# A convolution inside a fused two-layer kernel: taps clipped to the image in place of a zero border, with another spread of TensorE's work over the stages

## The chip, the cores and the metric

The kernel runs on one core of a Trainium2 chip. The core has a matrix engine (TensorE, PE in the profile; its weight loads are listed apart as PEld), three engines for elementwise work (VectorE or DVE, ScalarE or ACT, GpSimd or POOL), an engine that only issues transfers (SyncE or SP), and DMA queues. Matmuls write to PSUM, an accumulation memory that TensorE, VectorE and ScalarE can use; everything else lies in SBUF, and both have 128 partitions. The metric is the device time of one execution in microseconds (us).

## What is computed

The input x holds 32 images of 256 channels and 32 x 32 pixels, in fp32. Two layers follow, each one normalized first and added to its input:

```python
# cut to what matters; _gn is a GroupNorm of 32 groups (8 channels each) over channels of a group and all pixels
x = x + conv3x3(_gn(x), weight, bias)        # 256 -> 256 channels, padding 1; operands rounded to fp16, result rounded to fp16
                                             # (the kernel works per image, each on its own)
h = _gn(x)                                   # second layer, an involution
y = relu(bn(w1 @ h))                         # 256 -> 64 channels
w = w2 @ y + b2                              # 49 weights for each pixel and each of 16 groups
x = x + sum over the 7 x 7 taps of w[tap, group] * h[pixel + tap]     # zero outside of the image
```

The convolution of one image is, for each half of the rows (nt) and each half of the output channels (mh), a sum of 18 matmuls: 9 taps times 2 halves of the input channels (kh). Each has 128 x 128 weights and up to 512 columns, which are 16 rows of 32 pixels.

## The kernel before

Work is cut into stages: one stage is an image b, a block k of 8 rows (four blocks), a set v of columns of the 7 x 7 window (two sets), and a set d of its rows (two sets), so 16 stages per image. In a stage VectorE and GpSimd multiply the involution's weights with shifted pixels, and TensorE sums these products one stage later. Beside this, the "front" of a later image goes on in small steps: it is a Python generator, and each `yield` ends what it does in one stage. A front takes over 30 stages, so the fronts of two or three images are under way at once.

```python
xq = const.tile([P, CH, H0, H0], F16, name="xq")      # H0 = 34: a border of one pixel
nc.gpsimd.memset(xq, 0.0)
...
MORE = 1
CONV = (0, 9, 0, 9)                                   # matmuls in each of four stages

def front(b):
    ...                                               # sums, means, squares, variances of the first norm
    gn.apply(lambda h: xq[:, h, PAD0 : PAD0 + H, PAD0 : PAD0 + W], xt)        # ScalarE (L243)
    yield
    ...
    for s in range(1, 4 * len(units) + 3):            # units: (nt, mh), four of them
        u, i = divmod(s, 4)
        if u < len(units):
            nt, mh = units[u]
            if i == 1:
                pc = ps_c.tile([P, NT], F32, tag="pc", name="pc")
            for n in range(sum(CONV[:i]), sum(CONV[: i + 1])):
                kh, k = divmod(n, K0 * K0)
                i0, j0 = divmod(k, K0)
                nc.tensor.matmul(                     # L288
                    pc,
                    wq[:, kh, k, mh * P : (mh + 1) * P],
                    xq[:, kh, nt * RT + i0 : nt * RT + i0 + RT, j0 : j0 + W],
                    start=n == 0, stop=n == CH * K0 * K0 - 1,
                )
        ...                                           # a stage after a unit's last matmul: q (VectorE, L302), qb (ScalarE, L304);
                                                      # then x += qb (GpSimd, L306), then the unit's sum (ScalarE)
        yield
    gn.means()                                        # group means: matmuls into pg (L203)
    gn.squares(xt)                                    # ScalarE
    yield
    yield
    gn.variances()                                    # pg again
    yield
    gn.scales()                                       # reciprocal on VectorE
    gn.apply(lambda h: xn[:, h]..., xt)               # xn, ScalarE (L231 to L243)
    yield
    for r in range(0, H // 4, 2):
        ...                                           # four 128 x 128 transposes of xn into pt (L326), a copy (L330), four transfers
        if r % 4 == 0:
            yield MORE                                # go on in this stage, after the other fronts
        else:
            yield
            if r == 2:
                yield
    load_pixels(b, 0)
    yield
    ...                                               # projection to y: matmuls into py (L346), ReLU on ScalarE (L354)
    yield
...
# in each stage, in this order: products of this stage (VectorE, GpSimd; L417), sums of the stage before (TensorE; L471),
# the end of a block (ScalarE copy L482, transposes back L488, addition on VectorE L497, L500),
# in every second stage the involution's weights for two stages on (pw, TensorE; L380; a copy for GpSimd, ws, ScalarE L389), then:
for b in list(fronts) * 2:
    due = n - FRONT - b * per + 1
    ...
    while b in fronts and done[b] < due:
        got = next(fronts[b], fronts)
        if got is fronts:
            fronts.pop(b)
        elif got == MORE:
            break
        done[b] += 1
```

The sums and the involution's weights are matmuls with 32 output columns, four side by side in the array (in the profile 128*32, 96*32 and 65*32). Convolution, transposes and group means use all 128 columns (128*128), and the projection 64.

Of the kernel before, what the change touches and what calls it, by code (L numbers as in the profile page):

```python
# [8 lines left out]
F16 = mybir.dt.float16  # L9
# [4 lines left out]
P = 128  # L14
B, C, H, W = 32, 256, 32, 32
N = H * W
NT = 512
RT = NT // W
CH = C // P
K0, PAD0 = 3, 1  # L20
H0 = H + 2 * PAD0
K1, PAD1 = 7, 3
TAPS = K1 * K1
CR = 64
# [33 lines left out]
def tile_quant_conv_then_involution(  # L58
# [15 lines left out]
    nc = tc.nc  # L74
    PSUM = bass.MemoryType.PSUM

    const = ctx.enter_context(tc.tile_pool(name="const", bufs=1))
# [9 lines left out]
    def load_x(b):  # L87
        xt = xpool.tile([P, CH, N], F32, tag="x", name=f"x_{b}")
        for h in range(CH):
            nc.sync.dma_start(xt[:, h], x[b, h * P : (h + 1) * P])  # L90
        return xt
# [49 lines left out]
            )  # L141
        shift.append(s)

    xq = const.tile([P, CH, H0, H0], F16, name="xq")
    nc.gpsimd.memset(xq, 0.0)
    eps = const.tile([P, 1], F32, name="eps")
    nc.gpsimd.memset(eps, GN_EPS)
    three_halves = const.tile([P, 1], F32, name="three_halves")
# [99 lines left out]
                    scale=rstd[:, one],  # L248
                )

    MORE = 1

    CONV = (0, 9, 0, 9)

    def front(b):


        xt = x_tiles[b]
        gn = GroupNorm()
        gn.begin(1)  # L260
        for h in range(CH):
            gn.add_up(xt, 0, h, 0, N, AF.Identity)
        yield
        gn.means()
        gn.squares(xt)
        yield
        yield
        gn.variances()
        yield
        gn.scales()  # L270
        yield
        yield

        gn.apply(lambda h: xq[:, h, PAD0 : PAD0 + H, PAD0 : PAD0 + W], xt)
        yield
        gn = GroupNorm()
        gn.begin(N // NT)
        units = [(nt, mh) for nt in range(N // NT) for mh in range(CH)]
        for s in range(1, 4 * len(units) + 3):
# [3 lines that stand above are left out]
                if i == 1:  # L283
                    pc = ps_c.tile([P, NT], F32, tag="pc", name="pc")
                for n in range(sum(CONV[:i]), sum(CONV[: i + 1])):
                    kh, k = divmod(n, K0 * K0)
                    i0, j0 = divmod(k, K0)
                    nc.tensor.matmul(  # L288
                        pc,
                        wq[:, kh, k, mh * P : (mh + 1) * P],  # L290
                        xq[:, kh, nt * RT + i0 : nt * RT + i0 + RT, j0 : j0 + W],
                        start=n == 0,
                        stop=n == CH * K0 * K0 - 1,
                    )

            u, i = divmod(s - 4, 4)
            if 0 <= u < len(units) and i < 3:
                nt, mh = units[u]
                cols = slice(nt * NT, (nt + 1) * NT)
                if i == 0:  # L300
                    q = work.tile([P, NT], F16, tag="q", name="q", bufs=1)
                    nc.vector.tensor_scalar(q, pc, F16_MAX, -F16_MAX, ALU.min, ALU.max)  # L302
                    qb = work.tile([P, NT], F32, tag="qb", name="qb", bufs=1)
                    nc.scalar.activation(qb, q, AF.Identity, bias=bias_sb[:, mh : mh + 1])  # L304
                elif i == 1:
                    nc.gpsimd.tensor_tensor(xt[:, mh, cols], qb, xt[:, mh, cols], ALU.add)  # L306
                else:
                    gn.add_up(xt, nt, mh, nt * NT, (nt + 1) * NT, AF.Identity)
            yield
        gn.means()  # L310
        gn.squares(xt)
        yield
        yield
        gn.variances()
        yield
        gn.scales()
        xn = work.tile([P, CH, N], F32, tag="xn", name=f"xn_{b}", bufs=1)
        gn.apply(lambda h: xn[:, h].rearrange("p (r c) -> p r c", c=W), xt)
        yield

        xd = pixels[b] = dram.tile([W, H, C], F32, tag="xd", name=f"xd_{b}")
        for r in range(0, H // 4, 2):
            pt = ps_m.tile([P, 2, C], F32, tag="m", name="pt")
            for s in range(2):
                for h in range(CH):
                    nc.tensor.transpose(  # L326
                        pt[:, s, h * P : (h + 1) * P], xn[:, h, (r + s) * P : (r + s + 1) * P], ident
                    )
            xt4 = work.tile([P, 2, C], F32, tag="xt4", name="xt4")
            nc.scalar.copy(xt4, pt)  # L330
            for i in range(4):
                nc.sync.dma_start(xd[:, 4 * r + i : 4 * r + i + 5 : 4, :], xt4[i * W : (i + 1) * W])

            if r % 4 == 0:
                yield MORE
            else:
                yield
                if r == 2:
                    yield
        load_pixels(b, 0)  # L340
        yield

        py = ps_m.tile([P, NT], F32, tag="m", name="py")
        for kh in range(CH):
            for nt in range(N // NT):
                nc.tensor.matmul(  # L346
                    py[nt * CR : (nt + 1) * CR],
                    w1_sb[:, kh, :],
                    xn[:, kh, nt * NT : (nt + 1) * NT],
                    start=kh == 0,  # L350
                    stop=kh == CH - 1,
                )
        for nt in range(N // NT):
            nc.scalar.activation(  # L354
                y_pad[b % 2][:CR, nt * RT : (nt + 1) * RT, PAD1 : PAD1 + W],
                py[nt * CR : (nt + 1) * CR].rearrange("p (r c) -> p r c", c=W),
                AF.Relu,
                bias=bn_shift,
                scale=bn_scale,
            )  # L360
        yield

    def load_pixels(b, i):

        for r0, r1 in (((0, 7), (15, 22), (7, 15)), ((0, 14), (14, 22)))[i]:
            src = HELD[i][r0]
            for q in range(Q):
                nc.sync.dma_start(
                    xpix[i][q * W : (q + 1) * W, r0:r1], pixels[b][:, src : src + r1 - r0, :]
                )  # L370
# [146 lines left out]
    with tc.manual_schedule():  # L517
        fronts, done = {}, {}
        ending = iter(())
        acc = last = None  # L520
        pws = {}
        for n in range(FRONT, len(stages) + 3):
            if 0 <= n < len(stages):
                b, k, v, d = stages[n]
                now = stages[n], products(b, k, v, d, *pws[n // 2])
            else:
                now = None
            if last is not None:
                (b, k, v, d), prods = last
                if (v, d) == (0, 0):  # L530
                    acc = ps_acc.tile([P, NT], F32, tag="acc", name="acc")
                sums(acc, v, d, prods)
            next(ending, None)
            if last is not None and (v, d) == (len(COLS) - 1, len(DI) - 1):
                ending = finish(b, k, acc)
                next(ending)
            last = now
            b, at = divmod(n, per)
            if at == 0 and 0 <= b < B:
                load_pixels(b, 1)  # L540
            if 0 <= n + 2 < len(stages) and n % 2 == 0:
                pws.pop(n // 2 - 1, None)
                pws[n // 2 + 1] = weights(*stages[n + 2][:3])
            b, at = divmod(n - LOAD, per)
            if at == 0 and 0 < b < B:
                x_tiles[b] = load_x(b)
            b, at = divmod(n - FRONT, per)
            if at == 0 and 0 <= b < B:
                fronts[b] = front(b)
                done[b] = 0  # L550
            for b in list(fronts) * 2:
                due = n - FRONT - b * per + 1
                if b == 1:

                    due = min(due, max(0, 2 * (due - HOLD)))
                while b in fronts and done[b] < due:
                    got = next(fronts[b], fronts)
                    if got is fronts:
                        fronts.pop(b)
                    elif got == MORE:  # L560
                        break
                    done[b] += 1


# [34 lines left out]
```

## Time and profile before

| | |
|---|---|
| time, median of 3 runs | 2789.55 us (2781.03 to 2789.92) |
| span of the profiled execution | 2788.2 us |
| granted TensorE clock, mean | 0.990 |
| sums (L471), matmul records | 14080 |
| convolution (L288) | 2304 matmuls, 556.3 us busy |
| involution weights (L380) | 14336 records, 440.7 us busy |
| VectorE products (L417) | 2006.3 us and 334.9 us |
| GpSimd products (L417) | 704 instructions, 2407.2 us |
| GpSimd additions (L306) | 128 instructions, 164.5 us, 184.6 us idle ahead of them |
| DMA | 292.60 MB, mean 105 GB/s |

Groups of matmuls overlap in time, so their busy times may not be added. An fp32 matmul leaves two records. "Idle before" is the time in which an engine stood still just ahead of the instructions of a group; what ended it is named behind the arrow. Matmuls are pipelined, and their ends are modelled: the distance from one start to the next says what a matmul costs in a stream, while its length says how long it is under way.

### The profile page before, as it was taken

What the parts mean: (1) busy time and instruction counts of PE and PEld (TensorE: products, weight loads), DVE (VectorE), ACT (ScalarE), POOL (GpSimd) and SP (SyncE); (2) the same over time, 40 slices, a digit from 0 to 9 for tenths busy, and PEclk for the clock granted to TensorE, in tenths of its full rate; (3) what the DMA queues carried; (4) which work ended last, traced back from release to release, by engine and by line L of the source; (5) the groups of instructions that cost most, each with busy time, mean ns of one, the idle gap of its engine ahead of it and who ended that gap; (6) DMA issues with size and microseconds to landing.
All of it is one profiled execution on the core that took longest, in us unless ns stands there. A gap on an engine that the chain in (4) does not pass through costs nothing.

```text
span 2788.2 us, 73320 instructions
## 1 busy us (share of the span) xinstructions
PE 2685.1 (96%) x32320; PEld 1323.7 (47%) x32320; DVE 2484.6 (89%) x1451; ACT 1052.4 (38%) x2179; POOL 2575.8 (92%) x857
## 2 busy tenths in 40 slices
PE   4899999999999999999999999999999999999998
PEld 2444455454444444545444444444444444554443
DVE  1699999999999999999999999999999999999898
ACT  5434343433343433343333333343433343434220
POOL 2799999999999999999999999999999999999997
PEclk8999999999999999999999999999999999999999
DMA  2555343454343454343554343554344553434440
GB/s 84 121 122 117 95 105 93 114 126 112 92 113 85 118 130 108 89 112 89 122 129 101 87 112 98 122 129 93 95 103 107 122 119 94 104 90 101 111 115 16
DMA packets 99853, 292.60 MB, mean 105 GB/s; under 512 B 21389, under 2 KB 62349, under 8 KB 86990
## 3 DMA queue, kind: packets, MB, share of 16 engines
q1 hardware_dynamic: 99534, 287.93, 42.4%
q8 instruction: 252, 4.13, 0.7%
q14 instruction: 67, 0.55, 0.1%
HBM read 220.73 MB, written 67.11 MB: 103 GB/s over the span
## 4 chain that ended last, share of the span: by engine, by line
PE 85%; ACT 10%; issue 2%; POOL 1%; DMA 1%; DVE 1%; POOLq 0%; SPq 0%; ACTq 0%; DVEq 0%
PE acc L471 46%; PE pc L288 18%; PE pw L380 13%; ACT xn L243 3%; PE pt L326 2%; PE py L346 2%; PE acc L488 2%; ACT xq L243 1%; POOL pg L417 1%; ACT w L234 1%; PE pg L203 1%; ACT off L242 1%; ACT rstd L241 1%; ACT qb L304 1%; ACT u L236 1%
## 5 line engine op out<-in xcount | busy, mean ns | idle before, releaser
L417 POOL TENSOR_TENSOR pg<-ws,xpix 96x2048 f32<-96x2048 f32 (+2 forms) x704 | 2407.2, 3452 | 14.5 <-PE acc L471 4.8
L417 DVE TENSOR_TENSOR pa<-pw,xpix 128x4096 f32<-128x4096 f32 (+7 forms) x832 | 2006.3, 2446 | 216.1 <-PE acc L471 171.6
L471 PE MATMUL acc<-pa,shift 128*32 128x512 f32 (+3 forms) x7680 | 1563.8, 569 | 7.9 <-DVE pa L417 7.8
L471 PE MATMUL acc<-pg,shift 128*32 128x512 f32 (+1 forms) x5248 | 1503.2, 599 | 5.5 <-POOL pg L417 5.5
L471 PEld LDWEIGHTS acc<-pa,shift 128*32 128x32 f32 (+1 forms) x7680 | 394.9, 110 | 558.8 <-issue 497.8
L288 PE MATMUL pc<-xq,wq 128*128 128x512 f16 x2304 | 556.3, 387 | 15.6 <-ACT xq L243 10.7
L471 PEld LDWEIGHTS acc<-pg,shift 128*32 128x32 f32 (+1 forms) x5248 | 457.1, 111 | 162.0 <-issue 141.5
L471 PE MATMUL acc<-pb,shift 128*32 128x512 f32 (+1 forms) x1152 | 532.4, 599 | 1.5 <-DVE pb L417 1.5
L380 PEld LDWEIGHTS pw<-w_sb,y 65*32 65x32 f32 x14336 | 413.2, 110 | 139.9 <-issue 133.8
L380 PE MATMUL pw<-w_sb,y 65*32 65x112 f32 x14336 | 440.7, 259 | 0.0
L389 ACT COPY ws<-pw 128x448 f32<-128x448 f32 (+1 forms) x256 | 135.7, 530 | 693.5 <-PE pw L380 507.3
L288 PEld LDWEIGHTS <-wq 128*128 128x128 f16 x2304 | 221.2, 100 | 300.8 <-issue 81.5
L306 POOL TENSOR_TENSOR x<-qb,x 128x512 f32<-128x512 f32 x128 | 164.5, 1285 | 184.6 <-ACT qb L304 171.7
L417 DVE TENSOR_TENSOR pb<-pw,xpix 128x1536 f32<-128x1536 f32 x192 | 334.9, 1744 | 0.0
L482 ACT COPY ob<-acc 128x512 f32<-128x512 f32 x128 | 74.9, 585 | 435.6 <-PE acc L471 434.3
L330 ACT COPY xt<-pt 128x512 f32<-128x512 f32 x128 | 75.0, 586 | 221.9 <-PE pt L326 125.7
L195 ACT ACTIVATE junk<-x 128x512 f16<-128x512 f32 (+1 forms) x192 | 148.1, 771 | 10.0 <-POOL x L306 5.6
L195 ACT ACTIVATE junk<-x,mean 128x1024 f16<-128x1024 f32 x128 | 147.1, 1149 | 4.1
L326 PE MATMUL pt<-ident,xn 128*128 128x128 f32 x512 | 86.8, 283 | 47.4 <-ACT xn L243 45.3
L302 DVE TENSOR_SCALAR q<-pc 128x512 f16<-128x512 f32 x128 | 87.4, 683 | 48.8 <-PE pc L288 48.8
L471 PEld LDWEIGHTS acc<-pb,shift 128*32 128x32 f32 (+1 forms) x1152 | 111.8, 110 | 7.8 <-DVE pb L417 4.2
L220 ACT ACTIVATE s<-pg,eps 128x2 f32<-128x2 f32 x64 | 16.8, 262 | 238.5 <-PE pg L203 238.5
(51 smaller groups left out, 1023.9 us busy)
## 6 DMA issues: line engine op xcount, KB each, us to landing
xpix<-xd SPq DMA_DIRECT2D x256, 256.0 KB, 10.1
xpix<-xd SPq DMA_DIRECT2D x256, 224.0 KB, 5.6
xpix<-xd SPq DMA_DIRECT2D x128, 448.0 KB, 6.9
x<-in_x SPq DMA_DIRECT2D x64, 512.0 KB, 3.6
xd<-xt SPq DMA_DIRECT2D x512, 64.0 KB, 1.7
out<-x SPq DMA_DIRECT2D x32, 640.0 KB, 3.1
out<-x SPq DMA_DIRECT2D x32, 384.0 KB, 2.5
wf<-in_w SPq DMA_DIRECT2D x2, 1152.0 KB, 8.5
```

What stands on the lines that cost most here:

```text
L195: nc.scalar.activation(junk[:, n0:n1], src[:, h, n0:n1], func, bias=bias, accum_out=self.sums[:, part, h : h + 1])
L243: nc.scalar.activation(dst(h), src[:, h].rearrange("p (r c) -> p r c", c=W), AF.Identity, bias=off[:, one], scale=rstd[:, one],)
L288: nc.tensor.matmul(pc, wq[:, kh, k, mh * P : (mh + 1) * P], xq[:, kh, nt * RT + i0 : nt * RT + i0 + RT, j0 : j0 + W], start=n == 0, stop=n ...
L302: nc.vector.tensor_scalar(q, pc, F16_MAX, -F16_MAX, ALU.min, ALU.max)
L306: nc.gpsimd.tensor_tensor(xt[:, mh, cols], qb, xt[:, mh, cols], ALU.add)
L326: nc.tensor.transpose(pt[:, s, h * P : (h + 1) * P], xn[:, h, (r + s) * P : (r + s + 1) * P], ident)
L330: nc.scalar.copy(xt4, pt)
L380: nc.tensor.matmul(pw[q * W : (q + 1) * W, r // 4, o : o + K1 * G], y_pad[b % 2][:, ROWS[k][r], s : s + W], w2_sb[:, dj, :], start=True, s ...
L389: nc.scalar.copy(ws[:p], pw[:p, 1, : 4 * K1 * G].rearrange("p (r m) -> p r m", r=4))
L417: eng.tensor_tensor(o, win, xin, ALU.mult)
L471: nc.tensor.matmul(acc[t * W : (t + 1) * W, cols], shift[v][:p], moving, start=(v, d, i) == (0, 0, 0), stop=(v, d, i) == (len(COLS) - 1, l ...
L482: nc.scalar.copy(ob, acc.rearrange("p (r c) -> p r c", c=C))
```

## The change

The border of zeros around the normalized fp16 input xq goes, with its clearing. Each of the nine taps now covers only those pixels whose input lies inside of the image: a tap that looks up or down leaves out one row in the half that has that edge, a tap that looks left or right leaves out one column (its matmul has rows of 31). The order of the taps changes so that the first and the last of the 18, which start and end the accumulation, are the middle tap, which covers all pixels.

With it comes another spread of the front's work. The 18 matmuls of a unit are issued as 6, 4 and 8 in three stages, not as 9 and 9 in two. The variances come one stage after the squares, not two; the transposes come one group per stage in four stages, not two groups in each of two stages; the projection comes in the stage of the pixel loads, one earlier; and the loop over the fronts is simpler.

```diff
@@ -18,7 +18,6 @@
 RT = NT // W
 CH = C // P
 K0, PAD0 = 3, 1
-H0 = H + 2 * PAD0
 K1, PAD1 = 7, 3
 TAPS = K1 * K1
 CR = 64
@@ -141,8 +140,7 @@
             )
         shift.append(s)
 
-    xq = const.tile([P, CH, H0, H0], F16, name="xq")
-    nc.gpsimd.memset(xq, 0.0)
+    xq = const.tile([P, CH, H, W], F16, name="xq")
     eps = const.tile([P, 1], F32, name="eps")
     nc.gpsimd.memset(eps, GN_EPS)
     three_halves = const.tile([P, 1], F32, name="three_halves")
@@ -248,9 +246,8 @@
                     scale=rstd[:, one],
                 )
 
-    MORE = 1
-
-    CONV = (0, 9, 0, 9)
+
+    CONV = (0, 6, 4, 8)
 
     def front(b):
 
@@ -264,14 +261,14 @@
         gn.means()
         gn.squares(xt)
         yield
-        yield
         gn.variances()
         yield
         gn.scales()
         yield
         yield
-
-        gn.apply(lambda h: xq[:, h, PAD0 : PAD0 + H, PAD0 : PAD0 + W], xt)
+        yield
+
+        gn.apply(lambda h: xq[:, h], xt)
         yield
         gn = GroupNorm()
         gn.begin(N // NT)
@@ -283,12 +280,17 @@
                 if i == 1:
                     pc = ps_c.tile([P, NT], F32, tag="pc", name="pc")
                 for n in range(sum(CONV[:i]), sum(CONV[: i + 1])):
-                    kh, k = divmod(n, K0 * K0)
-                    i0, j0 = divmod(k, K0)
+
+
+                    k = n if n < K0 * K0 else CH * K0 * K0 - 1 - n
+                    kh, k = n // (K0 * K0), (k + K0 * K0 // 2) % (K0 * K0)
+                    di, dj = k // K0 - PAD0, k % K0 - PAD0
+                    r0, r1 = max(nt * RT, -di), min((nt + 1) * RT, H - di)
+                    c0, c1 = max(0, -dj), min(W, W - dj)
                     nc.tensor.matmul(
-                        pc,
+                        pc.rearrange("p (r c) -> p r c", c=W)[:, r0 - nt * RT : r1 - nt * RT, c0:c1],
                         wq[:, kh, k, mh * P : (mh + 1) * P],
-                        xq[:, kh, nt * RT + i0 : nt * RT + i0 + RT, j0 : j0 + W],
+                        xq[:, kh, r0 + di : r1 + di, c0 + dj : c1 + dj],
                         start=n == 0,
                         stop=n == CH * K0 * K0 - 1,
                     )
@@ -310,7 +312,6 @@
         gn.means()
         gn.squares(xt)
         yield
-        yield
         gn.variances()
         yield
         gn.scales()
@@ -330,15 +331,8 @@
             nc.scalar.copy(xt4, pt)
             for i in range(4):
                 nc.sync.dma_start(xd[:, 4 * r + i : 4 * r + i + 5 : 4, :], xt4[i * W : (i + 1) * W])
-
-            if r % 4 == 0:
-                yield MORE
-            else:
-                yield
-                if r == 2:
-                    yield
+            yield
         load_pixels(b, 0)
-        yield
 
         py = ps_m.tile([P, NT], F32, tag="m", name="py")
         for kh in range(CH):
@@ -548,17 +542,14 @@
             if at == 0 and 0 <= b < B:
                 fronts[b] = front(b)
                 done[b] = 0
-            for b in list(fronts) * 2:
+            for b in list(fronts):
                 due = n - FRONT - b * per + 1
                 if b == 1:
 
                     due = min(due, max(0, 2 * (due - HOLD)))
                 while b in fronts and done[b] < due:
-                    got = next(fronts[b], fronts)
-                    if got is fronts:
+                    if next(fronts[b], fronts) is fronts:
                         fronts.pop(b)
-                    elif got == MORE:
-                        break
                     done[b] += 1
```

## The prediction

> **What bounds the kernel now.** I read the page's shares first, then the chain of work that ended last, then the costliest groups.
>
> ```profile
> PE 2685.1 (96%) x32320; PEld 1323.7 (47%) x32320; DVE 2484.6 (89%) x1451; ACT 1052.4 (38%) x2179; POOL 2575.8 (92%) x857
> ...
> PE 85%; ACT 10%; issue 2%; POOL 1%; DMA 1%; DVE 1%; POOLq 0%; SPq 0%; ACTq 0%; DVEq 0%
> PE acc L471 46%; PE pc L288 18%; PE pw L380 13%; ACT xn L243 3%; PE pt L326 2%; PE py L346 2%; PE acc L488 2%; ACT xq L243 1%; POOL pg L417 1%; ACT w L234 1%; PE pg L203 1%; ACT off L242 1%; ACT rstd L241 1%; ACT qb L304 1%; ACT u L236 1%
> ...
> L326 PE MATMUL pt<-ident,xn 128*128 128x128 f32 x512 | 86.8, 283 | 47.4 <-ACT xn L243 45.3
> ```
>
> TensorE carries the chain, GpSimd and VectorE are close behind, and one wait stands out: the pixel transposes (L326) wait 45.3 us in all for the normalized input xn. A busy TensorE need not be one at its peak, so I looked at the steady state. The projection (py, L346) starts 84.21 us after that of the image before, image after image. One such period, by busy time of each engine and by what TensorE waited for:
>
> ```profile
> 1200.00:1284.20 84.20, 82.76 (x1016) 41.23 (x1012) 77.49 (x46) 32.78 (x68) 80.15 (x27) 1.00 0.44 107
> PE pt L326 <- ACT xn L243: 1.4, 1, 1.4
> ```
>
> The first line's columns after the length are PE, PEld, DVE, ACT and POOL. TensorE has no idle time in a period but 1.4 us, all of it that wait. So the time is 32 times TensorE's work in a period, plus this wait, plus a start of 77 us before the first projection and a tail of about 104 us after the last. VectorE (77.5) and GpSimd (80.2) fit in, GpSimd with 4 us to spare.
>
> What TensorE's work consists of is seen in the timeline of TensorE (start, length, instructions):
>
> ```profile
> 1214.09 0.59 PE L471 MATMUL acc<-pg,shift 128*32 128x512 f32 x1
> 1214.61 0.66 PE L488 MATMUL acc<-ident,ob 128*128 128x128 f32 x4
> 1215.10 0.28 PE L203 MATMUL pg<-sums,avg 128*128 128x2 f32 x2
> 1215.24 2.14 PE L288 MATMUL pc<-xq,wq 128*128 128x512 f16 x9
> 1217.32 0.62 PE L471 MATMUL acc<-pa,shift 128*32 128x512 f32 x2
> ...
> 1224.47 0.90 PE L471 MATMUL acc<-pg,shift 96*32 96x512 f32 x2
> 1225.30 0.33 PE L326 MATMUL pt<-ident,xn 128*128 128x128 f32 x1
> 1227.01 0.55 PE L326 MATMUL pt<-ident,xn 128*128 128x128 f32 x3 [1.38 <-ACT xn L243]
> 1227.39 2.15 PE L288 MATMUL pc<-xq,wq 128*128 128x512 f16 x9
> 1229.38 0.60 PE L326 MATMUL pt<-ident,xn 128*128 128x128 f32 x4
> 1229.91 0.62 PE L471 MATMUL acc<-pa,shift 96*32 96x512 f32 x2
> ```
>
> Work on all 128 columns (transposes, group means, convolution) comes in islands between sums and weights that use the array as four strips of 32 columns. The starts of single records give what an island costs beside its work. Within the sums the last record of a row of eight is followed after 409 ns; before an island after 523 to 525, so 115 ns are lost going in. A convolution matmul is followed by the next after 217 ns, but by the sums after 309, so 92 are lost going out: **207 ns per island**. An island that begins with a transpose loses 56 more (165 instead of 109 ns after the first).
>
> The nine matmuls of a convolution run show a second thing. Median distances to the next start are 216, 229, 215, 216, 229, 216, 215, 229 ns: the taps whose rows begin at an odd column (j0 = 1) cost 13 ns more. Sixteen rows of one extra fp16 pair are 32 elements, 6% of 512, and 6% of 213 ns is 13. So rows seem to be charged by pairs touched: 17 instead of 16.
>
> **What the Trainium skill says.** "TensorE: Matmul & The Clock Gate", Back-to-back issue gap: N/2.4 + 2.5 ns for a warm matmul alone, 215.8 for 512 columns; the trace has 216, so the convolution is charged by its columns, and the page says nothing of the 229. "TensorEngine Tiling (Array Packing)", Key Properties: "Changing tiling mode (not just tile) drains the TensorE"; the 115 + 92 ns agree. "PSUM — Partial Sum Buffer", Specifications: an 8-byte line, and any non-contiguous access pattern slows matmuls significantly. That bears on the new outputs of 31 columns; here L488 writes runs of 32 with gaps for three blocks in four and takes 109 ns between starts either way, but no run in this trace starts at an odd column.
>
> **The change part by part.**
>
> *Clipped taps.* A run is nine taps on half an image; there are 8 runs per image (2 halves, 2 output halves, 2 input halves). Three taps of a run lose one row of 16: 32 of 512 columns, 13 ns each, 40 ns. The three middle taps, at an odd column because of the border, now begin at column 0: 229 to 216, 39 ns. The six side taps have rows of 31, which still touch 16 pairs, so I count no gain for them; counted by element it would be 6 x 16 columns, 39 ns more. Sum: 79 ns x 8 = -0.63 us per image, **-20 us** over 32 (-30 by element).
>
> *More islands.* Nine taps in each of two stages become 6, 4 and 8 in three, and transposes and group means no longer share a stage with convolution in each case. Counting islands along the two instruction orders: 254 before, 466 after, 212 more; in the steady state 8 and 15 per image. The seven are four short convolution runs, one of transposes alone and two of group means alone. 212 x 0.207 = 43.9 us; two more islands per image begin with transposes, 64 x 0.056 = 3.6. All of it is on TensorE, which has no idle time to hide it: **+47.5 us**.
>
> *The xn wait.* Before, xn is computed in the stage just ahead of the first transposes: ScalarE waits for the copy of the weights (ends 1222.2), needs 4.75 us for the scales and the two halves of xn (ends 1226.95), and TensorE is there at 1225.3. After, the variances come a stage earlier, and so do scale and xn; in the frame of this period VectorE's reciprocal can come at 1215.1, right after its products, and xn is done at 1220.0. The transposes are one stage earlier too, but behind 2.6 us of sums and 1.6 us of weights of that stage, at about 1221.2. Margin 1.2 us, so the wait goes: **-45 us**. This is a choice: I trust the queues to keep their present leads.
>
> *No border, no clearing of it, dense xq.* One memset of 2 us at the start, beside other work; the ScalarE write of xq is off the path. The start changes by 2 us at most, the tail not at all, as it has no convolution.
>
> Sum: -20 + 47.5 - 45 = -17.5 us; from 2789.6 to **2772**. Per image that is 83.6 us.
>
> Does GpSimd allow it? Its products for one stage ended at most 0.3 us ahead of the sums three times in the period I followed. Moving every stage's start by the figures above, the work of GpSimd between two additions of the convolution result (21.4, 21.4, 18.7, 18.8 us) meets TensorE stretches of 21.8, 23.2, 20.4 and 18.3. It falls behind by 0.5 us in one, has it back in the next two, and no product comes late, with 0.2 us to spare at the tightest. VectorE's tightest is 0.8. I add no wait but widen the range upward.
>
> **Rivals.**
>
> *Odd columns slow the output.* A tap with input one column to the left writes columns 1 to 31, from input that starts even, so every pair straddles two lines. That is a third of the convolution, 768 matmuls. If each line were written twice, each would take some 200 ns more: +154 us, about 2926. For it: the page on PSUM. Against: an odd input start to an even output costs only 13 ns today, so pairs can be shifted somewhere. I give it one in ten.
>
> *The wait stays in another place*: xn late again, or means and variances (a stage closer together) held up by ScalarE's squares, or products from GpSimd. One wait of 1.4 us per image leaves the gain of the clipping against the islands: about 2817. For it: GpSimd's small lead. Against: squares take 2.3 us plus a mean, and 4 us of TensorE work lie between.
>
> *Islands overlap better than counted*: the new ones follow weights rather than sums, and the loss going in may differ there. At half of the count: 2749.
>
> **Range and chances.** The three terms are each uncertain by 10 to 15 us; most of the weight lies between a side gain by element (2762) and a small new wait. I take 2752 to 2806. A change by 2% is 56 us: down to 2734 all must go well at once, 0.03; up to 2845 needs the odd columns, or the wait to come back doubled, 0.11; within, 0.86.
>
> **What will show it.** Starts of the convolution's matmuls: 216 for full taps, 202 for those of 15 rows, 216 for rows of 31 (209 if by element, over 300 if the odd column hurts). Islands: 15 per image with 115 and 92 ns around them. The L326 wait on xn: near zero. A projection every 83.6 us. I am wrong if an interval over 230 ns shows up in the convolution, or if TensorE has idle time at pg, pt, or the sums.

## The result and the profile after

The changed kernel takes **2762.44 us** (median of 6; 2760.99 to 2764.09) against 2789.58 for the kernel before: a ratio of 0.9908, 95% interval 0.9895 to 0.9921. The prediction was 2772, range 2752 to 2806. From the page of the kernel after, the shares, and the chain of work that ended last by engine and by line:

```profile
PE 2700.3 (98%) x32320; PEld 1226.3 (44%) x32320; DVE 2472.5 (90%) x1451; ACT 1047.1 (38%) x2179; POOL 2572.9 (93%) x856
...
PE 90%; ACT 5%; POOL 2%; DVE 1%; issue 1%; POOLq 0%; DMA 0%; SPq 0%; ACTq 0%; DVEq 0%
PE acc L465 50%; PE pc L290 18%; PE pw L374 14%; PE pt L327 2%; PE py L340 2%; PE acc L482 2%; POOL pg L411 2%; PE pg L201 2%; ACT xq L241 1%; DVE pa L411 1%; ACT qb L306 1%; ACT w L232 1%; ACT junk L193 1%; ACT rstd L239 0%; ACT u L234 0%
```

TensorE is busy longer (2700 in place of 2685 us) in a shorter span, and ScalarE's xn (3% before) is no longer among the lines of the chain that the page lists. The groups by line show where the wait went; the column behind the last bar is the idle time ahead of the group:

```profile
L290 PE MATMUL pc<-xq,wq 128*128 128x496 f16 (+3 forms) x2304 | 556.9, 380 | 18.5 <-ACT xq L241 15.2 <-DVE q L304 3.3
L327 PE MATMUL pt<-ident,xn 128*128 128x128 f32 x512 | 82.2, 283 | 1.1 <-ACT xt L331 1.1
```

The pixel transposes wait 1.1 us in place of 47.4. In a steady period (columns as in the prediction: length, then PE, PEld, DVE, ACT, POOL):

```profile
1061.60:1145.22 83.62, 83.46 (x1014) 37.99 (x1011) 77.11 (x46) 32.60 (x68) 80.17 (x27) 1.00 0.45 109
```

And all that TensorE waited for in another period:

```profile
PE pc L290 <- ACT xq L241: 0.2, 1, 0.2
```

The projection returns every 83.62 us. The timeline of TensorE in the stage where the transposes begin:

```profile
1121.38 1.72 PE L374 MATMUL pw<-w_sb,y 65*32 65x112 f32 x64
1123.03 0.66 PE L327 MATMUL pt<-ident,xn 128*128 128x128 f32 x4
1123.52 1.00 PE L290 MATMUL pc<-xq,wq 128*128 128x480 f16 x4
1124.45 0.62 PE L465 MATMUL acc<-pa,shift 96*32 96x512 f32 x2
```

Transposes and four matmuls of the convolution follow the weights in one island, and the four transposes run without a break.

Busy time hides part of the waits, as the ends of matmuls are modelled. So I kept a ledger: for each matmul record of TensorE the distance to the start of the next, added up by what the record is, over 24 steady images. It sums to the period, with waits in it.

| us per image | before | after | clip alone (exp. 1) | spread alone (exp. 1) | early variances (exp. 2) | clip + early variances (exp. 6) |
|---|---|---|---|---|---|---|
| sums | 47.22 | 46.85 | 47.54 | 46.85 | 46.88 | 47.19 |
| involution weights | 12.05 | 12.98 | 12.05 | 12.98 | 12.24 | 12.24 |
| convolution | 16.26 | 16.31 | 15.63 | 16.94 | 16.26 | 15.63 |
| transposes to pixels | 3.59 | 2.01 | 3.43 | 2.01 | 1.99 | 1.99 |
| transposes of a block | 2.19 | 2.29 | 2.04 | 2.30 | 2.20 | 2.03 |
| group means | 1.03 | 1.30 | 1.03 | 1.30 | 1.20 | 1.20 |
| projection | 1.87 | 1.87 | 1.87 | 1.87 | 1.87 | 1.87 |
| period | 84.21 | 83.62 | 83.58 | 84.25 | 82.63 | 82.15 |

The loss going into an island is booked with the record ahead of it, so more islands show under weights too. Before to after: the transposes lose 1.58 us, which is the wait; the convolution loses 0.63 of columns and gains 0.68 of loss going out; weights, means and block transposes gain 1.30; the sums lose 0.37. Together -0.59 us per image.

### The profile page after: what moved, and what is told of

Its sections match the earlier page's. It is cut to its first block, busy times and chain, and to the rows that moved or that the text cites. A ratio compares the mean times of both kernels' runs of the same rounds, so it can differ in the third digit from the quotient of the medians.

```text
span 2761.9 us, 73318 instructions
## 1 busy us (share of the span) xinstructions
PE 2700.3 (98%) x32320; PEld 1226.3 (44%) x32320; DVE 2472.5 (90%) x1451; ACT 1047.1 (38%) x2179; POOL 2572.9 (93%) x856
## 4 chain that ended last, share of the span: by engine, by line
PE 90%; ACT 5%; POOL 2%; DVE 1%; issue 1%; POOLq 0%; DMA 0%; SPq 0%; ACTq 0%; DVEq 0%
PE acc L465 50%; PE pc L290 18%; PE pw L374 14%; PE pt L327 2%; PE py L340 2%; PE acc L482 2%; POOL pg L411 2%; PE pg L201 2%; ACT xq L241 1%; DVE pa L411 1%; ACT qb L306 1%; ACT w L232 1%; ACT junk L193 1%; ACT rstd L239 0%; ACT u L234 0%
## 5 line engine op out<-in xcount | busy, mean ns | idle before, releaser
L465 PE MATMUL acc<-pg,shift 128*32 128x512 f32 (+1 forms) x5248 | 1480.8, 599 | 6.1 <-POOL pg L411 6.1
L465 PEld LDWEIGHTS acc<-pa,shift 128*32 128x32 f32 (+1 forms) x7680 | 380.2, 110 | 802.8 <-issue 748.5
L290 PE MATMUL pc<-xq,wq 128*128 128x496 f16 (+3 forms) x2304 | 556.9, 380 | 18.5 <-ACT xq L241 15.2
L465 PEld LDWEIGHTS acc<-pg,shift 128*32 128x32 f32 (+1 forms) x5248 | 357.3, 110 | 63.4 <-issue 49.4
L290 PEld LDWEIGHTS <-wq 128*128 128x128 f16 x2304 | 215.2, 100 | 293.9 <-issue 119.3
L482 PEld LDWEIGHTS acc<-ident,ob 128*128 128x128 f32 x512 | 53.6, 140 | 108.1 <-issue 82.1
L306 ACT ACTIVATE qb<-q,bias_sb 128x512 f32<-128x512 f16 x128 | 92.5, 723 | 10.6 <-DVE q L304 10.6
```

The lines of the kernel that those rows point to most:

```text
L290: nc.tensor.matmul(pc.rearrange("p (r c) -> p r c", c=W)[:, r0 - nt * RT : r1 - nt * RT, c0:c1], wq[:, kh, k, mh * P : (mh + 1) * P], xq[: ...
L465: nc.tensor.matmul(acc[t * W : (t + 1) * W, cols], shift[v][:p], moving, start=(v, d, i) == (0, 0, 0), stop=(v, d, i) == (len(COLS) - 1, l ...
L482: nc.tensor.transpose(po[:, h, :, r, :], ob[:, r, h * P : (h + 1) * P], ident)
```

## The experiments

**1. The two parts apart.** First the clipped taps in the old stages:

```diff
# kernel before, plus only:
-    xq[:, kh, nt * RT + i0 : nt * RT + i0 + RT, j0 : j0 + W]     (border of zeros; CONV stays (0, 9, 0, 9))
+    xq[:, kh, r0 + di : r1 + di, c0 + dj : c1 + dj]               (dense xq, output rows and columns cut likewise, taps in the new order)
```

> The kernel before with clipped taps alone; stages as before (9 and 9, eight islands of 128-column work per image). My theory: only the convolution's columns change, so a projection every 84.21 - 0.63 = 83.58 us, the wait of the first transposes for xn stays at 1.4 us per image, time 2769 us. Rival: a TensorE that is faster only waits longer for xn, the wait grows to 2.0 us, and the time stays at 2789.

Measured: 2767.36 us (ratio 0.9945, 0.9925 to 0.9964), period 83.58. The convolution lost just the 0.63 us. TensorE's waits in a period of this kernel:

```profile
PE pt L328 <- ACT xn L242: 1.2, 1, 1.2
```

So the wait stays, a little shorter. The transposes lost 0.16 us and the block transposes 0.15; the sums gained as much (47.22 to 47.54).

Then the spread alone, with the border put back:

```diff
# kernel after, but
-    xq = const.tile([P, CH, H, W], F16, name="xq")               (clipped taps)
+    xq = const.tile([P, CH, H0, H0], F16, name="xq")             (zero border, nine full taps in the old order)
```

> The changed kernel with the zero border and full taps put back; 6, 4, 8 and 15 islands per image stay. My theory: the islands cost 1.56 us per image and the wait for xn is gone, so a projection every 84.25 us; with the shorter start of the changed kernel, 2782 us. If the shorter start comes from the clipped taps and not from the order of stages, 2790.

Measured: 2784.32 us (0.9994, 0.9985 to 1.0004), period 84.25. In the steady state the spread is worth nothing: 1.58 us of wait are exchanged for 1.62 us of islands and other rows of the ledger. The gain of the change per image is that of the clipped taps.

**2. The wait by itself.** Only the second norm's variances are moved:

```diff
         gn.squares(xt)
         yield
-        yield
         gn.variances()
         ...
         gn.apply(lambda h: xn[:, h]..., xt)
         yield
+        yield
```

> The kernel before with one thing moved: the second norm's variances, scales and xn come one stage earlier, the transposes stay where they were. My theory: the wait of 1.4 us per image goes, the group means of that stage now are an island of their own (0.2 us), so a projection every 83.0 us, 2752 us. Rival: GpSimd's products, which came just in time, now come late; TensorE idles at the sums in place of the transposes, and the time falls by less than 15 us.

Measured: 2736.55 us (0.9831, 0.9811 to 0.9851), more than expected; period 82.63. In the kernel before, the prediction's lines show the first transpose at 1225.30 and the next at 1227.01. The same place with this one change:

```profile
1117.50 0.66 PE L326 MATMUL pt<-ident,xn 128*128 128x128 f32 x4
1117.99 2.15 PE L288 MATMUL pc<-xq,wq 128*128 128x512 f16 x9
```

Two waits went. The one on xn was 1.6 us (the four transposes with it took 2.10 us, now 0.49), not the 1.38 that the idle time shows; the modelled end of the transpose ahead of it covers the rest. And the sums just ahead took 3.84 us before and take 3.55 now. The first sums of GpSimd's products there, and these products themselves, before:

```profile
1221.47 0.90 PE L471 MATMUL acc<-pg,shift 96*32 96x512 f32 x2
1214.35 7.35 POOL L417 TENSOR_TENSOR pg<-ws,xpix 96x2048 f32<-96x2048 f32 x2
```

And such sums with early variances:

```profile
1113.96 0.60 PE L471 MATMUL acc<-pg,shift 96*32 96x512 f32 x2
```

The 0.90 holds two records whose starts lie 0.28 us apart: one strip ran 0.3 us behind the three others, as its product tile from GpSimd ended at 1221.70, after the sums began at 1221.45. The group means as an island of their own cost 0.31 us: the stage that has them grew from 10.39 to 10.70 us. Why that is more than 0.207 was not tested. One reason may be that in the kernel before the first sum of that stage starts on the free strip 0.17 us before those that wait for the end of the weights, and that an island in between prevents this.

**3. Islands by themselves**, once where waits are and once where none are left:

```diff
-    CONV = (0, 9, 0, 9)
+    CONV = (0, 5, 4, 9)
```

On the kernel before:

> The kernel before with the 18 convolution matmuls as 5, 4 and 9 in three stages in place of 9 and 9: the same work in four more islands per image, and nothing else moved. My theory: 4 x 0.207 us per image more, a projection every 85.04 us, 2816 us. Rival: islands behind weights cost little, and the time stays within 8 us of before.

Measured: 2779.21 us (0.9974, 0.9965 to 0.9982): four islands more, and *a little faster*. The period is 84.07. Its timeline at the transposes:

```profile
1129.84 1.05 PE L288 MATMUL pc<-xq,wq 128*128 128x512 f16 x4
1134.39 0.33 PE L326 MATMUL pt<-ident,xn 128*128 128x128 f32 x1
1135.28 0.55 PE L326 MATMUL pt<-ident,xn 128*128 128x128 f32 x3 [0.56 <-ACT xn L243]
```

The four matmuls of the convolution now lie ahead of the transposes, so TensorE works where it waited: the wait went from 1.38 to 0.56. In the ledger the islands cost 0.82 us (weights +0.41, convolution +0.41; 0.83 expected) and the block transposes grew by 0.10, while the transposes lost 0.82 and the sums 0.25. My expectation forgot that work put in front of a wait is free. The rival (cheap islands) gives the same time, so the same edit was made on the kernel with early variances:

> The kernel with early variances (2736.6 us), which has no wait left, with the matmuls as 5, 4 and 9 in place of 9 and 9: the same four islands more as in the run that split the kernel before so and got faster. My theory: islands cost the same wherever they lie, and there they were paid for out of the waits for xn and for GpSimd; here nothing is left to pay with, so 4 x 0.207 us per image more, a projection every 83.45 us, 2763 us. Rival: islands behind weights are cheap; the time stays below 2745.

Measured: 2761.34 us (0.9901, 0.9886 to 0.9916), period 83.60: with no wait on xn ahead, four islands cost 0.97 us per image. The rival falls.

**4. Nine and nine in the changed kernel.**

```diff
-    CONV = (0, 6, 4, 8)
+    CONV = (0, 9, 0, 9)
```

> The changed kernel with the 18 matmuls as 9 and 9 in place of 6, 4 and 8: four islands fewer per image, the rest of the stages as changed. My theory: as the changed kernel has no wait left, all of 4 x 0.207 us comes back, a projection every 82.8 us, 2737 us. Rival: TensorE comes to the first transposes 1 us earlier in that stage and waits for xn again; the period falls by less than 0.4 us and the time stays above 2750.

Measured: 2750.96 us (0.9864, 0.9847 to 0.988), period 83.03, so 0.59 less, not 0.83. No wait on xn came back; I had miscounted. In the traces there are 15 islands per image after and 12 here, but one of the three stood behind the projection: of the four short runs one shared its island with transposes, which stay, and the one behind the projection saves only a change between 64 and 128 columns (about 0.1 us). Two islands at 0.207 and this make 0.5 of the 0.59 us. The other part of what is missing to 2737 us lies mostly in the start: at a mean clock of 0.990 the seventh copy of the weights begins at 147.37 us here and at 141.97 in the changed kernel.

**5. What a row costs.** On the kernel with early variances, rows of 36 with the image at column 2, so that left and right taps begin at odd columns:

```diff
-xq = const.tile([P, CH, H0, H0], F16, name="xq")     ... j0 : j0 + W
+xq = const.tile([P, CH, H0, 36], F16, name="xq")     ... j0 + 1 : j0 + 1 + W
```

> The kernel with early variances (2736.6 us), with a border of two columns on the left in place of one (rows of 36), so that the middle taps begin at an even column and the six side taps at an odd one. If rows are charged by the fp16 pairs that they touch, the distances to the next start are 229, 216, 229 for left, middle and right taps, six of nine at 229 in place of three: 0.31 us more per image, 2746 us. If it is the middle tap or the odd column inside of the rows of 34 that is slow, nothing changes or all taps take 216.

Measured: 2745.38 us (0.9844, 0.9829 to 0.9859). The period is 82.95, 0.33 us longer. Of the nine distances of a run the first eight have medians of 229, 217, 228, 229, 219, 231, 228, 215 ns (the ninth is the way out): the slow taps are now the side taps. In the changed kernel they are 215 to 217 for full rows and rows of 31, and 201 to 204 for taps with 15 rows, at odd output columns (left taps) as at even ones (right taps). So in all these cases the cost of a row follows the number of fp16 pairs that it touches, and neither the odd output column nor the gaps in the output cost anything here. The Trainium skill ("PSUM — Partial Sum Buffer", Specifications) says that any non-contiguous pattern slows matmuls significantly; for these rows of 31 the measurement says otherwise, and it decides. A few positions take 226 to 227 with 16 rows, and one 213 with 15: there the convolution begins an island.

**6. Both parts that help, together**: the kernel before, with clipped taps and with early variances.

> The kernel before with clipped taps and with the second norm's variances, scales and xn one stage earlier; convolution as 9 and 9. My theory: with no wait left the clipped taps give their full 0.63 us per image, a projection every 82.0 us against 82.63 without them, 2716 us. Rival: GpSimd (80.2 us of work per image) now sets the pace; the sums wait for its products, the period stays above 82.4 and the time above 2728 us.

Measured: **2718.65 us** (0.9748, 0.9733 to 0.9763): better than both kernels. The period is 82.15, between the two expectations: of 0.63 us, 0.48 arrive. The ledger's sums hold 0.31 more than without the clipping, the block transposes 0.17 less. The timeline again has a strip behind (0.75 in place of 0.60):

```profile
1107.32 0.60 PE L473 MATMUL acc<-pa,shift 96*32 96x512 f32 x2
1107.33 0.75 PE L473 MATMUL acc<-pg,shift 96*32 96x512 f32 x2
```

GpSimd has 80.2 us of work in a period of 82.15, and here does not stand still ahead of any addition of the two I followed. To see whether it sets the pace, two of its four additions per image were moved:

```diff
-    nc.gpsimd.tensor_tensor(xt[:, mh, cols], qb, xt[:, mh, cols], ALU.add)
+    (nc.vector if u % 2 == 0 else nc.gpsimd).tensor_tensor(xt[:, mh, cols], qb, xt[:, mh, cols], ALU.add)
```

> The kernel with clipped taps and early variances (2718.7 us), with two of the four additions of the convolution's result per image moved from GpSimd to VectorE: those just ahead of the two stages whose sums took 3.70 and 3.80 us in place of 3.55. My theory: the missing 0.15 us per image of the clipping went into waits for GpSimd's last product tile; now both sums take 3.55 us, 0.15 us of the 0.4 goes to a longer wait for the convolution's input xq, a projection every 81.9 to 82.0 us, 2710 to 2714 us. Rival: VectorE's products come later by the addition and TensorE waits for them; the time is 2718 or more.

Measured: 2718.6 us (0.9769, 0.9755 to 0.9782), period 82.15: nothing gained (the ratio is higher because the kernel before ran at 2781.91 beside it; see the last section). The sums did go back to 3.55 and 3.57 us in the two stages, so GpSimd was late there. But in both stages the time came back elsewhere. Ahead of the transposes the rival came true: the sums began 1.67 us after the weights in place of 1.53, at 1104.74, when VectorE's product, now behind an addition, had just ended at 1104.69:

```profile
1100.28 4.41 DVE L419 TENSOR_TENSOR pa<-pw,xpix 96x4096 f32<-96x4096 f32 x1
1103.07 1.72 PE L382 MATMUL pw<-w_sb,y 65*32 65x112 f32 x64
1104.74 0.62 PE L473 MATMUL acc<-pa,shift 96*32 96x512 f32 x2
```

In the other stage the convolution waits for xq:

```profile
1074.39 1.61 PE L382 MATMUL pw<-w_sb,y 65*32 65x112 f32 x45
1079.47 0.66 PE L490 MATMUL acc<-ident,ob 128*128 128x128 f32 x4
1080.28 2.07 PE L290 MATMUL pc<-xq,wq 128*128 128x512 f16 x9 [0.16 <-ACT xq L242]
```

From those weights to that convolution it takes 5.89 us here; without the addition moved too (1077.10 to 1082.99), in the kernels before and after, and in every run so far. A stretch that keeps its length whatever the sums in it take is likely set by something beside it, here perhaps ScalarE's chain from the copy of the weights to xq. Two more runs took this up, with two buffers for xq and its computation one stage earlier:

```diff
-    xq = const.tile([P, CH, H, W], F16, name="xq")
+    xqs = [const.tile([P, CH, H, W], F16, name=f"xq_{i}") for i in range(2)]      # xq = xqs[b % 2]
-        yield
         gn.apply(lambda h: xq[:, h], xt)
         yield
+        yield
```

> The kernel with clipped taps and early variances (2718.7 us), with two buffers for the convolution's input xq, which ScalarE then makes one stage earlier. In six kernels so far the stretch from the weights ahead of the sums to the first convolution matmul after xq took 5.89 us, whatever the sums in it took; my theory is that ScalarE's chain to xq sets it. Then TensorE is bound there by what comes next, GpSimd's late tile (sums of 3.80 in place of 3.55 us): the stretch falls by 0.07 us only, a projection every 82.08 us, 2716 us. Rival: it falls to 5.57 us, and the time to 2708 us or less, because GpSimd only looked late.

Measured: 2716.69 us (0.9749, 0.9726 to 0.9773), period 82.11. The stretch is 5.83 us, and the sums in it still take 3.80: GpSimd is next in line, as expected.

> The same with two of the four additions per image on VectorE as well. My theory: with both causes gone the stretch takes 5.57 us, a projection every 81.83 us, 2708 us. Rival: another wait takes their place (VectorE, now with 80.4 us of work per image), and the time stays at 2718.

Measured: 2714.25 us (0.9745, 0.9726 to 0.9764), period 82.11. The stretch falls to its bare work, 5.57 us, but in the stage ahead of the transposes the weights now last 1.94 in place of 1.53 us until the sums begin, and the profile names VectorE:

```profile
PE acc L473 <- DVE pa L419: 0.2, 1, 0.2
```

VectorE now has 80.4 us of work, and the additions delay its products. The rival was right that the wait moves. The four versions with clipping and early variances lie within 5 us of each other: TensorE's work fills nearly all of the period, and GpSimd or VectorE follows 2 us behind.

## Why the prediction was right, and where it was off

- **What bounds it**: right. But "no idle time in a period but 1.4 us" was wrong: the ledger shows 1.6 us at the transposes, 0.29 in the sums ahead of them and 0.32 at the stretch to xq. The last is in every kernel up to the two with a second xq buffer.
- **Clipped taps**: -0.63 us per image, as worked out; rows of 31 give nothing, the choice made there.
- **More islands**: 1.56 us per image predicted, 1.62 in the run with the spread alone (weights +0.93, convolution +0.68, means +0.27, block transposes +0.11, less the 0.37 of the sums, part of which is booking and part the wait gone).
- **The xn wait**: right that it goes, and why: xn ends 1.38 us ahead of the first transpose (1.2 predicted; 1121.65 and 1123.03 in the period above). Its size was 1.6, not 1.4.
- **GpSimd**: right that no product comes late in the changed kernel. In the kernel before, one did (experiment 2), which the prediction missed, and the sums of the two kernels with clipped taps in the old stages show the same sign. How long the period is does not decide it: it is 84.21 us in the kernel before and 83.62 in the changed one.
- **The sum**: per image the three terms give -0.63 + 1.56 - 1.4 = -0.47 us, a period of 83.74. The 83.6 of the prediction is -17.5 us over 32 images, -0.55 each, and that total counts fewer islands than 7 per image. The measured -0.59 lies nearer to it because the wait was 1.58 us in place of 1.4; that the period fits so closely is in part luck. "32 times TensorE's work plus 77 plus 104" is not the time either: between 32 projections lie 31 distances, the first of 76.7 us, and the tail is 108 us. The differences that the prediction works with do not suffer from it. And 2762 us, its figure for side taps charged by element, is what was measured, by chance: those taps gained nothing.
- **The start**: the term that came out otherwise in the two profiles. "The start changes by 2 us at most": the seventh copy of the weights (ScalarE) begins at 150.69 us before and at 141.97 after, 8.7 us earlier. That, with 30 images at 0.59 less, makes the 26.3 us between the spans. The transfers of the first image's pixels are issued 9 us earlier. SyncE's queue before, after, and in the kernel before with 5, 4 and 9 matmuls (experiment 3):

```profile
79.01 16.89 SPq L368 DMA_DIRECT2D xpix<-xd  x20
69.74 16.12 SPq L362 DMA_DIRECT2D xpix<-xd  x20
75.53 16.67 SPq L368 DMA_DIRECT2D xpix<-xd  x20
```

In the changed kernel the first transposes do not wait for xn and their groups follow stage by stage. But that is not the whole of it. The third kernel has the old order, its first transposes wait as before (1.48 and 1.45 us), and still its seventh copy begins at 143.84, 6.9 us ahead of the kernel before.

The granted clock differs between these profiles. In the kernel before it was low among the first transposes and where the sums begin. Nine matmuls of the convolution between the first transposes, before and in that third kernel:

```profile
67.84 4.05 PE L288 MATMUL pc<-xq,wq 128*128 128x512 f16 x9
66.67 2.15 PE L288 MATMUL pc<-xq,wq 128*128 128x512 f16 x9
```

Two stretches before (PE busy is the first number after the length; the clock stands behind the five engines):

```profile
80.00:90.00 10.00, 8.90 (x125) 5.11 (x126) 3.30 (x3) 6.45 (x15) 1.28 (x1) 1.00 1.03 228
90.00:100.00 10.00, 6.16 (x41) 1.36 (x37) 6.17 (x8) 5.67 (x12) 9.88 (x4) 0.67 1.03 219
```

And after, where the low clock fell earlier:

```profile
80.00:90.00 10.00, 10.00 (x129) 6.00 (x130) 5.46 (x3) 1.15 (x3) 5.41 (x2) 0.62 1.04 222
90.00:100.00 10.00, 8.99 (x126) 3.82 (x121) 8.30 (x13) 5.58 (x12) 10.00 (x4) 1.00 0.97 245
```

Over the first 140 us the mean clock is nearly the same, 0.89 before and 0.90 after, a difference of 1.4 us of full clock; so its amount does not explain 8.7 us, but what it fell on may. At the seventh copy the spread alone is 7.8 us ahead of the kernel before, the clipped taps alone 1.7, but the low clock fell in other places there as well. What share is the clock's, and what the transfers', stays open. The last section gives a reason to think that at one and the same clock the start gains no more than the 2 us that were predicted.

The rivals: the odd column did not hurt; the wait did not stay; islands after weights are not cheap. Of the signs of being wrong none came: in the steady state of the changed kernel no distance within the convolution exceeds 228 ns, and the only wait of TensorE that the profile names in the period looked at is the 0.2 us for xq.

## What to carry to other kernels

Before counting what a change adds to the busiest engine, find its waits: work put in front of a wait is free until the wait is used up, and the same work costs its full price once the wait is gone (four islands: 0.14 us gained per image in the one case, 0.97 lost in the other). Read waits from distances between starts, as lengths that are modelled can cover them: four transposes in 2.10 us in place of 0.49, or one of four strips that ends later than the rest. And when three engines are within a few per cent of each other, expect that a wait removed shows the one behind it; a stretch that keeps its length whatever is in it points to another engine that sets it.

## What was not expected of the hardware

The executions of the kernel before fall into steps: 2780 to 2782 us where the mean granted clock was 0.994, 2783 to 2786 at 0.992, and 2788 to 2790 at 0.990 or 0.991. The changed kernel has 2761 to 2762 at 0.994 and 2763 to 2764 at 0.991, so its steps lie closer together. At 0.994 for both, the change is worth some 19 us, close to the 17.5 of the prediction and to 30 x 0.59 us; the rest of the 27 between the medians goes with the clock. From 140 to 2600 us the clock is full in both profiles, so what is missing of it lies in the start or the tail. No execution of these two kernels at 0.994 was profiled.
